# Layer 0 of a sparse graph stack: another order for the sign check, the ranges, the turned weights and the reciprocal

## The chip, the core and the metric

The kernel runs on one NeuronCore of a Trainium2 chip. A core has four engines that compute, each with its own instruction stream: TensorE (PE, matrix products and transposes through the array; its weight loads are shown as PEld), VectorE (DVE), ScalarE (ACT) and GpSimd (POOL). SyncE (SP) issues most of the transfers between the chip's memory (HBM) and the on-chip memory (SBUF); GpSimd issues the gathers. TensorE writes into PSUM, from where ScalarE and VectorE read. The engines meet at semaphores only; each works through its own instructions in the order in which the program lists them.

The metric is the device time of one execution in microseconds (us), the median of several runs; less is better.

## The reference

Four graph layers follow one another, each with a residual and a layer norm over rows of 512 numbers. The graph has 2708 nodes, and `adj` is a 2708 x 2708 matrix with about four entries per row besides its diagonal, all positive. Cut to what matters, with `ln` for the layer norm:

```python
# layer 0
e2 = (adj @ x) * (diag + 1)
x = ln(x + (x - e2) @ w0 + b0)
# layer 1: attention from two score columns and gates from the neighbour sums
h = x @ W_sa;  s = h @ a_left, h @ a_right
e = where(adj != 0, exp(-leaky_relu(s_i + s_j)), 0)
x = ln(x + sigmoid(gate_a * (e @ h) / (sum(e) + 1e-5) + gate_b * (adj @ (x @ W_gc) + b)))
# layer 2
inc = adj + (adj > 0) / sqrt(count of the row)
x = ln(x + (inc @ x) / sum(inc))
# layer 3: adj scaled by the degrees on both sides
x = ln(x + tanh(D A D x @ W.T + b))
```

## The kernel before

The kernel does not multiply by the dense matrix. It finds the entries of each block of columns of the transposed matrix, makes lists of them, gathers the rows of x that they name, and adds them with small matrix products. Where a list could not hold what was found, or a value was negative, a dense program would run instead; with this input it doesn't. All that the change touches is the phase for layer 0 inside `sparse_stack`, written as an order by hand (`manual_schedule`): each engine works through the instructions in exactly the order of the Python calls.

Two tilings run through this phase. The search and the sums work on *blocks*: NB = 24 blocks of R = 113 nodes. The projections and norms work on *windows*: KB = 22 windows of 128 rows. Blocks are smaller than windows, so in some steps no new window is complete. `window_at` maps a step to its window: steps 1 to 7 have windows 0 to 6, step 8 has none, 9 to 16 have 7 to 14, 17 has none, then 18 on.

The calls, with the line of the instruction in the profile:

- `find(i, parts)` (VectorE): each block has four segments (parts); MAX8 (L858) takes the eight largest values of each row, MATCH_VALUE_LOAD and FIND_INDEX8 (L860) their places. Segments 0 and 1 have 678 columns, 2 and 3 have 565. `search(n)` does the next n parts of a running list that starts at block 3; at a block's last part it also does `count` and issues the load of the block three further on.
- `negatives(i)` (ScalarE, L845): the sign check, one pass over the block's 2486 columns whose result (`negs`) is read only at the end of the phase. It must be listed before the load that overwrites the block.
- `count(i)` (VectorE, L872 to L882): the totals of each row. `starts(i)`: TensorE adds the totals of the rows ahead (L889), then ScalarE makes `ahead` (L892), `middle` (L894) and `q` (L896). `ranges(i)` (VectorE, L901) and `mark(i)` (VectorE, L908) make the selection matrix, `fetch(i)` (TensorE, L913, eight products) applies it, `pick(i)` (VectorE, L922 to L953) reads the edges from it, and its four gathers (GpSimd, L600) follow, with `nvalue` (ScalarE, L956).
- `values0(i)` (ScalarE, L966 and L967, eight activations) spreads the edges' values, `sums0(i)` (TensorE, L613, `l0a`) adds the gathered rows, `inputs0(i)` (VectorE, L979 to L984) and `turn_u(i)` (TensorE L1064, ScalarE L1073) prepare the block for the projection.
- For a window: `project0` (TensorE, L584, `o_l`), `bias0` (VectorE, L990), `residual0` (VectorE L1000, ScalarE L1005 to L1009: mean, squares, root), `norm0` (VectorE's reciprocal L1017, then ScalarE L1018 and L1019). One step later, for layer 1: `turn_x` (TensorE L575, ScalarE L577), `next0` (TensorE L584, `h`, ScalarE L1034 to L1039, then copies of rows by SP), `rest0` (TensorE L584, `hb`) and `store0` (ScalarE L1052, then SP).
- Once in the phase, the score columns that `next0` needs beside W_sa: `gate_columns` (L805 to L811), `turn_w(k)` (TensorE L819, ScalarE L821, four of them), `times_a(k)` (TensorE, L827), `score_rows` (ScalarE, L835), `score_columns` (TensorE L841, ScalarE L842).
- `keep_busy(n)` (TensorE, L797, `unread`): products that nobody reads, two passes of 512 columns each.

The phase begins with blocks 0 to 2 by hand, and then a loop runs over steps k = 0 to 25. Step k lists, in this order: `turn_x`; `ranges`, `mark` and `fetch` of block m = k + 2; `project0` of the step's window; one part of the search; `pick(m)`; one part; `residual0` and `norm0`; `next0`; `values0(m)`; the rest of the search; `sums0(k+1)` and `inputs0(k+1)`; `rest0` with `starts(m+1)` in its middle; `turn_u(k+1)`. A step has four parts of the search; three steps ahead of each step without a window have five, the step without a window ("bare") two and the one after it three. At the end of a plain step k the search stands at block k + 3 complete, and after the three longer steps it is up to three parts further.

Transfers on SP are issued in program order. TensorE's and ScalarE's buffers for transposes (`ps_tr`) are two, those for products (`ps_o`) three.

Of the kernel before, what the change touches and what calls it, by code (L numbers as in the profile page):

```python
# [19 lines left out]
EC = 4  # L20
# [427 lines left out]
def sparse_stack(  # L448
# [29 lines left out]
    nc = tc.nc  # L478
    N, D = x.shape
# [3 lines left out]
    NB = (N + R - 1) // R  # L483
# [3 lines left out]
    WG = 2 * D + 8  # L487
# [160 lines left out]
    with ExitStack() as phase:  # L648
# [144 lines left out]
        def keep_busy(n):  # L793

            o = ps_o.tile([P, D], FP, tag="o", name="unread")
            for _ in range(n):
                nc.tensor.matmul(o, lhsT=ident, rhs=iota_t, start=True, stop=True)  # L797
# [46 lines left out]
        def negatives(i):  # L844
            nc.scalar.activation(  # L845
                nojunk, abuf[i % NA].rearrange("p b i -> p (b i)"), AF.Relu, scale=-1.0,
                accum_out=negs[:, i : i + 1],
            )
# [143 lines left out]
        def project0(w):  # L992
            o0[w] = project(window_uT.pop(w), wrows(w), w0_sb, f"l0_{w}")
# [145 lines left out]
            )  # L1139
        w_gc_sb = load_w(w_gc, "w_gc_sb", first)  # L1140
        spread_rows()
        keep_busy(3)
        clear_diagonal(2)
        pick(0)
        values0(0)
        find(1, (1,), values=False)
        find(1, (2, 3))
        count(1)
        starts(1)
        keep_busy(2)  # L1150
        find(2, (0,), places=False)
        ranges(1)
        mark(1)
        fetch(1)
        negatives(2)
        nc.scalar.memzero(gflat[1])
        nc.scalar.memzero(gflat[2][:, KB * R + 3 * D :])
        find(2, (0,), values=False)
        find(2, (1,), places=False)
# [6 lines left out]
        find(2, (2, 3))  # L1166
        load_adj(5)
        count(2)
        values0(1)
        sums0(0)  # L1170
        starts(2)
        keep_busy(2)
        inputs0(0)
        turn_u(0)
        load_diagonal(4, NB - 1 - 4, R)
        load_diagonal(NB - 1, 1, rows(NB - 1))
        ba_bc = load_row(ba, "ba_bc", n=1)
# [9 lines left out]
        def search(n):  # L1187

            for _ in range(min(n, len(to_find))):
                b, g = to_find.pop(0)  # L1190
                if g == 0:
                    negatives(b)
                find(b, (g,))
                if g == 1 and b + 1 < NB:
                    clear_diagonal(b + 1)
                if g == NG - 1:
                    count(b)
                    if b + NA < NB:
                        load_adj(b + NA)
# [6 lines left out]
        for k in range(NB + 2):  # L1206
            m = k + 2
            w, wx, rest = window_at.get(k), window_at.get(k - 1), window_at.get(k - 1)
            bare = 2 < k < NB and w is None
            after = 2 < k < NB and wx is None  # L1210
            parts = 4
            if any(t not in window_at for t in (k + 1, k + 2, k + 3)) and 2 < k < NB - 4:
                parts = 5
            if bare:
                parts, rest = 2, None
            if after:
                parts, rest = 3, window_at[k - 2]
            if wx is not None and k <= NB:
                turn_x(wx)
            if m < NB:  # L1220
                ranges(m)
                mark(m)
                fetch(m)
            if w is not None:
                project0(w)
            if unstored:
                store0(unstored.pop())
            if k == 0:
                gate_columns()
                turn_w(0)  # L1230
                turn_w(1)
            search(1)
            if m < NB:
                pick(m)
                own[m] = load_own(m)
            if w is not None:
                bias0(w)
            search(1)
            if w is not None:
                residual0(w)  # L1240
            if k + 1 in window_at:
                load_window(window_at[k + 1])
            if w is not None:
                norm0(w)
            if k == 2:
                score_columns()
            if wx is not None and not bare:
                next0(wx)
            if m < NB:
                values0(m)  # L1250
            search(parts - 2)
            if k + 1 < NB:
                sums0(k + 1)
                inputs0(k + 1)
            if k + 2 == NB:
                worst = check_lists()
                for i in range(4):
                    load_own1(i)
            if k == 0:
                times_a(0)  # L1260
                turn_w(2)
                times_a(1)
            if k == 1:
                turn_w(3)
                times_a(2)
                times_a(3)
                score_rows()
            if bare:
                next0(wx)
            if rest is not None:  # L1270
                rest0(rest, lambda: turn_x(w) if k == NB else starts(m + 1) if m + 1 < NB else None)
                unstored.append(rest)
            elif m + 1 < NB:
                starts(m + 1)
            if k + 1 < NB:
                turn_u(k + 1)
            if k == NB:
                tell(worst)
                for i in range(4, NO):
                    load_own1(i)  # L1280
# [562 lines left out]
```

## Time and profile before

| | us |
|---|---|
| median of three runs | 1010.21 (1008.12 to 1011.41) |
| profiled execution, its own time | 992.9 |
| its span, first to last instruction | 991.2 |
| layer 0's phase within it | about 0 to 427 |
| mean granted TensorE clock | 0.968 |
| one plain step of layer 0, fetch to fetch | 15.74 |
| steps 5, 6, 7, 8, 9 | 16.30, 16.79, 16.95, 11.21, 14.50 |
| steps 14, 15, 16, 17, 18 | 16.31, 16.80, 16.95, 11.20, 13.66 |

A step's length is taken from the start of its first `fetched` product (L913) to that of the next step; the fetch of step k is that of block k + 2. Steps 0 to 3 begin at 40.17, 51.31, 69.97 and 89.95 us.

In the lines of the profile, L860 is line 860 of the kernel; `out<-in` names the tiles; xN is the number of instructions. In a timeline the first two numbers are the start and the length in us, and the brackets at the end say how long the engine had been idle before the instruction and whose end released it. A chain of waits is followed back from the last instruction to what each step had waited for.

### The profile page before, as it was taken

The page shows a single profiled execution, that of the slowest core. Times are in us where ns is not written, and L with a number is a line of the kernel's source. Part 1 is how long each engine was busy: PE and PEld are TensorE (multiplying, and loading weights), DVE is VectorE, ACT ScalarE, POOL GpSimd, SP SyncE. Part 2 cuts the span into 40 slices and gives each one's busy share as a digit, 9 for nine tenths or more (in the row PEclk, how much of TensorE's full clock was granted, in tenths as well). Part 3 has the DMA queues.
Part 4 walks back from the last instruction along what each step waited for, and adds up shares of the span by engine and source line. Part 5 has one row for each costly group of instructions (what it writes and reads, how often), then busy time and mean ns, then how long its engine had stood idle before and what let it go on. Part 6 is the DMA issues. An engine that isn't in the chain of part 4 may idle for free.

```text
span 991.2 us, 11201 instructions
## 1 busy us (share of the span) xinstructions
PE 899.3 (91%) x2973; PEld 494.5 (50%) x2973; DVE 686.4 (69%) x1803; ACT 530.0 (53%) x1219; POOL 473.0 (48%) x538
## 2 busy tenths in 40 slices
PE   7879999899998999999888888889888889999994
PEld 3335555555555555557666667633333334444441
DVE  7876888788887872138878878858787625655543
ACT  5765767667767664346776777415545412222222
POOL 3313131331313321046666767467777468776640
PEclk8979999999999999989999999989999999999998
DMA  9986877878778544378999998357777556555531
GB/s 237 302 210 173 210 216 195 236 220 223 213 214 219 163 131 123 118 231 294 299 317 283 323 299 279 93 158 211 221 219 211 159 151 181 169 169 163 168 109 32
DMA packets 133516, 201.70 MB, mean 203 GB/s; under 512 B 82456, under 2 KB 82502, under 8 KB 133445
## 3 DMA queue, kind: packets, MB, share of 16 engines
q0 software_dynamic: 36864, 111.73, 38.2%
q1 hardware_dynamic: 96581, 89.18, 31.8%
q8 instruction: 26, 0.43, 0.2%
q14 instruction: 45, 0.37, 0.1%
HBM read 181.83 MB, written 27.80 MB: 211 GB/s over the span
## 4 chain that ended last, share of the span: by engine, by line
PE 50%; DMA 16%; DVE 13%; ACT 10%; issue 6%; POOL 5%; SPq 0%; POOLq 0%; DVEq 0%; ACTq 0%
DMA gath<-table,source 15%; PE o_l L584 13%; PE l3a L613 8%; PE hb L584 5%; PE h L584 5%; PE l0a L613 4%; POOL gath L600 4%; PE l2a L613 4%; ACT s L967 2%; PE unread L1527 2%; DVE where_all L860 2%; ACT nojunk L845 2%; PE l1s L1404 2%; DVE rec_all L858 2%; PE fetched L913 1%
## 5 line engine op out<-in xcount | busy, mean ns | idle before, releaser
L600 POOL DMA_INDIRECT gath<-table,source x288 | 315.9, 1097 | 154.6 <-issue 64.0
L600 POOL DMA_INDIRECT gath<-in_x_dram,source x96 | 97.3, 1014 | 242.4 <-issue 204.5
L1404 PE MATMUL l1s<-gath,s 128*113 128x256 f32 (+3 forms) x384 | 96.6, 407 | 22.6 <-DVE l1b L1434 22.3
L613 PE MATMUL l2a<-gath,s_left 128*113 128x512 f32 (+1 forms) x192 | 95.7, 617 | 16.7 <-DMA gath<-table,source 14.5
L1404 PEld LDWEIGHTS l1s<-gath,s 128*113 128x113 f32 (+1 forms) x384 | 70.9, 189 | 48.4 <-DVE l1b L1434 29.7
L613 PE MATMUL l3a<-gath,s 128*113 128x512 f32 (+1 forms) x192 | 88.4, 602 | 3.6 <-DMA gath<-table,source 3.6
L584 PE MATMUL o_l<-shared,uT_l 128*113 128x512 f32 (+1 forms) x192 | 86.5, 593 | 0.7 <-ACT uT_l L577 0.7
L1414 PE MATMUL l1e<-gath,e 128*113 128x257 f32 (+3 forms) x384 | 87.0, 379 | 0.0
L613 PE MATMUL l0a<-gath,s 128*113 128x512 f32 (+1 forms) x192 | 86.3, 592 | 0.0
L584 PE MATMUL hb<-w_gc_sb,uT_x 128*128 128x512 f32 (+1 forms) x176 | 83.3, 601 | 0.0
L584 PE MATMUL o_l<-w_sb,uw 128*128 128x512 f32 (+1 forms) x176 | 82.4, 612 | 0.2
L584 PE MATMUL h<-w_sa_sb,uT_x 128*128 128x259 f32 (+1 forms) x352 | 81.0, 382 | 1.3 <-ACT w_sa_sb L842 1.3
L584 PEld LDWEIGHTS h<-w_sa_sb,uT_x 128*128 128x128 f32 (+1 forms) x352 | 64.8, 185 | 22.0 <-issue 8.0
L1414 PEld LDWEIGHTS l1e<-gath,e 128*113 128x113 f32 (+1 forms) x384 | 68.1, 177 | 15.2
L1762 ACT ACTIVATE y<-l3v,mv_l 113x512 f32<-113x512 f32 (+1 forms) x24 | 19.5, 813 | 87.3 <-DVE mv_l L1758 87.3
L613 PEld LDWEIGHTS l2a<-gath,s_left 128*113 128x113 f32 (+1 forms) x192 | 30.2, 179 | 71.7 <-DMA gath<-table,source 45.3
L584 PEld LDWEIGHTS o_l<-shared,uT_l 128*113 128x113 f32 (+1 forms) x192 | 33.9, 177 | 48.9 <-issue 47.1
L613 PEld LDWEIGHTS l3a<-gath,s 128*113 128x113 f32 (+1 forms) x192 | 32.6, 180 | 42.2 <-issue 39.3
L613 PEld LDWEIGHTS l0a<-gath,s 128*113 128x113 f32 (+1 forms) x192 | 33.8, 177 | 38.9 <-issue 37.7
L1291 DVE TENSOR_SCALAR s<-niota_r,nrow,edges 128x113 f32<-128x113 f32 x192 | 51.8, 349 | 0.0
L860 DVE FIND_INDEX8 where_all<-rec_all,shared 128x8 uint32<-128x678 f32 (+1 forms) x64 | 51.2, 800 | 0.0
L858 DVE MAX8 rec_all<-shared 128x8 f32<-128x678 f32 (+1 forms) x64 | 50.8, 795 | 0.0
(239 smaller groups left out, 1556.4 us busy)
## 6 DMA issues: line engine op xcount, KB each, us to landing
shared<-in_adj_dram SPq DMA_DIRECT2D x14, 1186.5 KB
table<-st SPq DMA_DIRECT2D x21, 514.5 KB
gath<-in_adj_dram SPq DMA_DIRECT2D x7, 1186.5 KB
shared<-table SPq DMA_DIRECT2D x16, 448.0 KB
gath<-in_x_dram SPq DMA_DIRECT2D x21, 256.0 KB
xi<-in_x_dram SPq DMA_DIRECT2D x23, 224.0 KB
table<-xr SPq DMA_DIRECT2D x23, 224.0 KB
table<-y SPq DMA_DIRECT2D x23, 224.0 KB
```

Of the source, the lines that this page charges most:

```text
L584: nc.tensor.matmul(o, lhsT=uT[:, f, :r], rhs=w[:, f, :], start=(f == 0), stop=(f == DB - 1))
L600: nc.gpsimd.indirect_dma_start(out=g[:, c, :n], out_offset=None, in_=src[:, :], in_offset=bass.IndirectOffsetOnAxis(ap=source[:, i, c : c ...
L613: nc.tensor.matmul(agg[:r, :], lhsT=s[:, c, :r], rhs=g[:, c, off : off + D], start=(c == 0), stop=(c == EC - 1),)
L845: nc.scalar.activation(nojunk, abuf[i % NA].rearrange("p b i -> p (b i)"), AF.Relu, scale=-1.0, accum_out=negs[:, i : i + 1],)
L858: nc.vector.max(out=top, in_=seg)
L860: nc.vector.max_index(out=where_all[:, i, g * 8 : (g + 1) * 8], in_max=top, in_values=seg)
L967: nc.scalar.activation(spread0[i][:, c, :], t, AF.Relu, bias=edges[:, i, c, 1:2], scale=nvalue[:, i, c : c + 1],)
L1291: nc.vector.tensor_scalar(s[:, c, :], niota_r, nrow[:, i, c : c + 1], edges[:, i, c, 1:2], op0=ALU.is_equal, op1=ALU.mult,)
L1404: nc.tensor.matmul(sum_s[i][:r, k, : at.stop - at.start], lhsT=s[:, c, :r], rhs=g[:, c, at], start=(c == 0), stop=(c == EC - 1),)
L1414: nc.tensor.matmul(sum_e[i][:r, k, k : k + at.stop - at.start], lhsT=e[:, c, :r], rhs=g[:, c, at], start=(c == 0), stop=(c == EC - 1),)
L1527: nc.tensor.matmul(o[:, :cols], lhsT=ident, rhs=bg_bc[:, :cols], start=True, stop=True)
L1762: nc.scalar.activation(y[:r, :], v[:r, :], AF.Identity, bias=mv[:r, 3:4], scale=mv[:r, 2:3])
```

## The change

No computation changes; instructions are listed elsewhere, and some are left out.

- Of the filler products, `keep_busy(3)` ahead of block 2's diagonal and the second `keep_busy(2)` are left out.
- `values0(0)` moves from ahead of block 1's last parts to after `starts(1)`; `values0(1)` from ahead of `sums0(0)` to after `turn_u(0)`.
- The zeroing of the second gather buffer leaves out the stretch that holds the windows.
- `gate_columns`, `turn_w(0)` and `turn_w(1)` move from step 0 to before `inputs0(0)`; `times_a(0)` and `turn_w(2)` go to the first part of step 0, `times_a(1)` and `turn_w(3)` to its end; `times_a(2)` and `times_a(3)` to before `project0` of step 1, `score_rows` after its `store0`, and `score_columns` from step 2 to the end of step 1.
- `negatives` no longer goes with a block's first part in `search`; each step k lists `negatives(k + 3)` after its `store0`.
- One part of the search moves ahead of `norm0` in steps with more than two parts.
- In a bare step `starts(m + 1)` is listed before `next0`.

```diff
         spread_rows()
-        keep_busy(3)
         clear_diagonal(2)
         pick(0)
-        values0(0)
         find(1, (1,), values=False)
         find(1, (2, 3))
         count(1)
         starts(1)
+        values0(0)
         keep_busy(2)
...
         negatives(2)
-        nc.scalar.memzero(gflat[1])
+        for a, b in ((0, EC * D), (EC * D + 4 * D + 12, EC * WG)):
+            nc.scalar.memzero(gflat[1][:, a:b])
...
         count(2)
-        values0(1)
         sums0(0)
         starts(2)
-        keep_busy(2)
+        gate_columns()
+        turn_w(0)
+        turn_w(1)
         inputs0(0)
         turn_u(0)
+        values0(1)
...
                 b, g = to_find.pop(0)
-                if g == 0:
-                    negatives(b)
                 find(b, (g,))
...
+            if k == 1:
+                times_a(2)
+                times_a(3)
             if w is not None:
                 project0(w)
+            if k == 0:
+                times_a(0)
+                turn_w(2)
             if unstored:
                 store0(unstored.pop())
-            if k == 0:
-                gate_columns()
-                turn_w(0)
-                turn_w(1)
+            if k + 3 < NB:
+                negatives(k + 3)
+            if k == 1:
+                score_rows()
             search(1)
...
+            if parts > 2:
+                search(1)
             if w is not None:
                 norm0(w)
-            if k == 2:
-                score_columns()
             if wx is not None and not bare:
                 next0(wx)
             if m < NB:
                 values0(m)
-            search(parts - 2)
+            search(parts - 3)
             if k + 1 < NB:
                 sums0(k + 1)
                 inputs0(k + 1)
+            if k == 1:
+                score_columns()
...
             if k == 0:
-                times_a(0)
-                turn_w(2)
                 times_a(1)
-            if k == 1:
                 turn_w(3)
-                times_a(2)
-                times_a(3)
-                score_rows()
             if bare:
+                starts(m + 1)
                 next0(wx)
-            if rest is not None:
+            elif rest is not None:
```

## The prediction

> **What bounds the kernel now.** I read the page, then a table of windows, the chain of waits in order of time, and the timeline of the steps that the chain named. The page's first part: TensorE is busy 91% of the span.
>
> ```profile
> PE 899.3 (91%) x2973; PEld 494.5 (50%) x2973; DVE 686.4 (69%) x1803; ACT 530.0 (53%) x1219; POOL 473.0 (48%) x538
> ```
>
> Layer 0 ends near 427 us. The windows say where TensorE is not full in it (busy us of PE, PEld, DVE, ACT, POOL, then granted clock, DMA share, GB/s):
>
> ```profile
> 20.00:40.00 20.00, 16.73 (x39) 7.05 (x38) 14.59 (x43) 14.80 (x29) 7.14 (x9) 0.76 1.04 333
> 60.00:80.00 20.00, 13.66 (x42) 7.38 (x40) 14.21 (x38) 12.88 (x30) 5.38 (x7) 0.74 0.66 174
> 100.00:120.00 20.00, 20.00 (x71) 11.41 (x70) 16.26 (x44) 14.46 (x38) 4.29 (x5) 1.00 0.75 195
> 160.00:200.00 40.00, 36.26 (x131) 20.85 (x130) 30.93 (x82) 28.28 (x69) 11.77 (x13) 0.96 0.80 224
> ```
>
> A plain step (100 to 120) is TensorE end to end; work taken off other engines there gains nothing. Two places have slack: the first 80 us, at three quarters of the clock, and the stretch around each step without a window (k=8, 17). The chain of waits (start, length) names ScalarE's sign check in the stretch:
>
> ```profile
> 65.90 1.87 PE w_a L827 x2
> ...
> 133.96 2.26 ACT nojunk L845 x2
> 150.55 2.26 ACT nojunk L845 x2
> 167.69 2.26 ACT nojunk L845 x2
> 174.95 2.35 ACT nojunk L845 x2
> 182.69 1.48 PE fetched L913 x8
> ```
>
> It returns at 272.79, 289.39, 306.54 and 313.79. The timeline of the start, with the idle time before each instruction and who ended it:
>
> ```profile
> 26.88 0.19 DVE L901 SCALAR_TENSOR_TENSOR rec_all<-ahead,far 128x32 f32<-128x32 f32 x1 [4.29 <-ACT ahead L892]
> ...
> 36.29 3.52 PE L797 MATMUL unread<-gath,ident 128*128 128x512 f32 x4
> ...
> 65.90 1.87 PE L827 MATMUL w_a<-w_saT,a_cols 128*2 128x512 f32 x2 [5.18 <-ACT w_saT L821]
> ...
> 80.19 2.02 PE L584 MATMUL h<-w_sa_sb,uT_x 128*128 128x259 f32 x8 [1.34 <-ACT w_sa_sb L842]
> ```
>
> VectorE stands 4.3 us for ranges(1), TensorE 5.2 us for the turned weight, 1.3 us for the score columns. And step 8's end, where the list of block 11 is late:
>
> ```profile
> 179.39 0.28 PE L889 MATMUL fetched<-totals,under 128*128 128x1 f32 x2
> ...
> 181.02 0.29 ACT L892 ACTIVATE ahead<-fetched,totals 128x1 f32<-128x1 f32 x1
> ...
> 182.69 1.48 PE L913 MATMUL fetched<-rec_all,q 128*128 128x96 f32 x8 [2.57 <-DVE q L908]
> ```
>
> **What the Trainium skill says.** "TensorE: Matmul & The Clock Gate", Part 1: an idle window of about 3.4 us halves the clock, a busy one restores it. The trace agrees: 512-column passes start 0.43 us apart, but 0.85 at 17 to 26, 37 to 40 and 68 to 74 us. The same page, architectural detail: ScalarE and VectorE are strict FIFO, matmuls keep their order; so each wait below stops all behind it, as the 4.29 us did. "ScalarE: Activation LUTs", What ACT_TABLE_LOAD costs: 0.833 ns per element; the zeroing of 4128 took 3.63 us, so 2048 is an estimated 1.9. "DMA: Bandwidth & Descriptors", Issuing engines are not separate DMA queues: both queues share 16 engines; their share is 1.04 at 20 to 40 us.
>
> **The start, part by part.** keep_busy(3) held TensorE from 20.94 to 26.4 while block 1's totals lay ready at 21.58; starts(1) waited, then ranges(1). It goes, and values0(0) (8 activations, 3.4 us) steps behind starts(1). For block 0 totals to ranges took 0.93 us (11.55 to 12.48), so ranges(1) comes at 22.6, after the find in between. But keep_busy(2), which stays, now runs at half clock, 4 x 0.85 from 22.3 to 25.7, ahead of fetch(1). So pick(1), 29.69 before, comes about 26.9. The smaller zeroing frees ScalarE 1.7 us earlier.
>
> From pick(1) VectorE is nearly full: its 6.5 us to count(2) and 2.2 us of inputs0(0) end at 35.6 instead of 38.38. The second keep_busy(2) (3.52 us) goes; gate_columns and two turn_w (9 small transposes, 1.3 us) take its place, hidden in TensorE's wait for inputs0(0). They need w_rows and w_sa, issued at 25.5 to 29.4; no row shows a landing; the DMA rate dips only near 37, so they land between 29.4 and 37. I take 34: first in their queue. TensorE now stands at gate_columns until then, with turn_u(0) and fetch(2) queued behind; at 37 turn_u(0) would be 1.2 us later. fetch(2): 36.6 instead of 40.17, at half clock (2.02 us as at 69.97), so pick(2) 38.8 instead of 41.25.
>
> Now ScalarE is full: from 34.8, two gate copies 0.35, three weight turns 1.7, turn_u 0.55, values0(1) 3.4 (moved here, past starts(2), so sums0(1) begins near 40.4 instead of 42.24), negatives(3) 2.3, nvalue 0.2, values0(2) 3.4, the fourth turn 0.6, starts(3) 1.2: 48.5, with 0.5 of mark, fetch(3) at 49.3 instead of 51.31. Two times_a (4 passes, 2.0) now precede project0(0), which so ends at 55.8, as before (55.9): here the move costs its full price. ScalarE's score_rows waits for them until 52.4; behind it stand nvalue(3) and residual0's statistics, needed at 56.8, so nothing is lost. But bias0(0) no longer waits for its window, since SP's loads begin 2.5 us sooner (load_adj(4) follows pick(1)'s gathers on POOL), so residual0(0) is at 56.0 instead of 57.46. The reciprocal, 3.4 us later as now (a 1.28 us table load in it), is at 59.4; one find (1.55) lies inside this wait. Behind it norm0 and values0(3) end at 64.1, the score copy 64.3, starts(4), mark(4) at 65.5 instead of 69.43: the 5.2 us stall is gone, since the turned weights were done 15 us before. turn_u, turn_x, fetch(4) at 66.2 instead of 69.97; clock still half as now; project0(1) ends at 72.9 if the clock returns at 70.7, 75.1 if at 74.1; next0(0) follows unbroken, 3.5: 76.4 or 78.6, before 82.21. Gain 3.6 to 5.8; a clock lost once more near 50 costs 1.4. Bounds 2 to 5.8; I take 5.0.
>
> **Plain steps.** The third part before the reciprocal: find 1.55 in a wait of 1.44, so 0.1 later. In step 3 (fetch 89.95) ScalarE waits 0.76 before ahead, and mark ends 0.85 before fetch: 1.6 us cover. Cost 0; without cover 0.1 a step. The sign check of a plain step stays where it was, after store0; no transfer moves.
>
> **The two stretches.** Steps 5, 6, 7 take 16.30, 16.79, 16.95 by their first fetch, against 15.74. Causes: the second sign check, 2.45 us, between values0 and ahead; and VectorE, 15.1 us of work plus 1.44 of waiting in step 6. After: the check sits behind store0, where ScalarE waits up to 4 us for residual0 anyway; VectorE's wait is filled. In steps 6 and 15 the third part ends a block (count 0.93), so the reciprocal is 1.05 late, within the 1.6; there the block load (2.9 us of SP's issue) also goes ahead of next0's row copies, which layer 1 alone reads. So 15.74, 15.82, 15.82: 0.56+0.97+1.13 = 2.66.
>
> Step 8, 11.21: values0(10) can begin at 174.95 instead of 177.21; starts(11) comes before next0, straight after sums0(9) (176.0), so ahead waits only for values0, 178.3, q 179.5, mark 180.0; TensorE's own row is fetch 1.13, sums 3.43, starts 0.15, h 3.5, turn_u 0.58 = 8.8. I take 9.0: 2.2. next0's h lies 0.15 later, copies then after ahead; their readers come in step 9.
>
> Step 9: three parts only, and the third ends block 12, so the reciprocal is at 8.8 after fetch (find 1.75, pick 1.85, bias 0.65, find 1.5, residual 0.7, find and count 2.4) instead of 8.46; nothing covers: 14.75 against 14.50, −0.25. Step 18: 8.65 against 7.62, −1.05.
>
> Stretch one 2.66+2.2−0.25 = 4.6; two, with 16.31, 16.80, 16.95, 11.20 and 13.66: 2.68+2.2−1.05 = 3.8.
>
> **Sum.** 5.0+4.6+3.8 = 13.4 us. All of it lies before layer 0's last rows, which layer 1 gathers, so it passes on. Span 991.2 to 977.8; the profiled execution 992.9 to 979.5; the three runs' median 1010.21, 17.3 above it, to 996.8. I say 997.
>
> **Rivals.** *Clock lost* (chance 0.15): with ten filler passes gone, TensorE stays at half clock through 40 to 54 us; sums0(1) takes 3.6 more, four times_a passes 1.8: 5.4, the start gains nothing. 8.4 left: 1002. For it: PEclk 0.76 despite filler. Against: the sums themselves make busy windows.
>
> *The start falls together* (0.08): every gap and half-clock loss after 36 us goes (2.1+5.2+1.3 idle, 3.4 of filler, 6 of clock: 18); with a third kept back 12, plus 8.4: 990. Against: between 40 and 80 us VectorE is busy 77%, ScalarE 66%, and each waits for the other.
>
> *Reciprocal* (slower, 0.05): the reciprocal queues behind a find and sometimes a count; if it came 2.3 us later in each of 18 steps, 0.75 over the 1.6 cover would eat 13.5 us and it begins to lose; at 2.6, 1014. Against: I count 0.1 and 1.05.
>
> *Swallowed* (0.06): layer 1's chain is 15% gathers; if these, not the rows, set its start, nothing changes: 1010. Against: the last rows' copies run up to 427, then layer 1 starts at once.
>
> **Numbers.** Forecast 0.66 (992 to 1001); faster 0.66+0.15+0.08 = 0.89, within 0.3% (3 us, about what this measurement can tell) 0.06, slower 0.05. The range 991 to 1003.5 takes in the forecast, the lost clock and half of the falling-together case; 0.15 is left out.
>
> **What shows it.** Right: nojunk gone from the chain; steps 5 to 7 at 15.8, 8 and 17 near 9; no 5.2 us wait at w_a; step 3's fetch near 85. Wrong: PEclk under 0.7 at 20 to 60, TensorE waiting at w_rows_t, plain steps over 15.9, or steps 9 and 18 over 16.

## The result and the profile after

| | before | after |
|---|---|---|
| median, us | 1011.41 (1007.05 to 1012.6, 7 runs) | 1001.58 (996.88 to 1003.22, 7 runs) |
| ratio, with 95% interval | | 0.991 (0.9885 to 0.9935) |
| profiled execution, its own time | 992.9 | 1001.58 |
| its span | 991.2 | 999.7 |

The change gains 9.8 us (6.6 to 11.6 by the interval) where 13.4 were forecast. The two profiled executions stand the other way round: that of before is quicker than all its timed runs. So the two spans can't be compared. Layer 0 can: its last `hb` product ends at 427.19 us before and at 419.34 after, 7.85 us earlier. Layers 2 and 3, which the change doesn't touch, take 128.5 and 191.5 us in the profile of before, 136.5 and 199.4 in that of after. Those 16 us get a paragraph of their own below.

The first part of the page, after: the engines' busy time, share of the span and instructions.

```profile
PE 898.5 (90%) x2963; PEld 498.5 (50%) x2963; DVE 685.7 (69%) x1803; ACT 527.9 (53%) x1220; POOL 472.4 (47%) x538
```

The table of windows, after (busy us of PE, PEld, DVE, ACT and POOL, then granted clock, DMA share, GB/s):

```profile
20.00:40.00 20.00, 15.81 (x49) 8.97 (x47) 16.41 (x46) 13.96 (x33) 7.42 (x9) 0.67 1.09 342
60.00:80.00 20.00, 16.00 (x57) 10.29 (x56) 15.23 (x43) 15.03 (x38) 4.42 (x5) 0.83 0.69 188
100.00:120.00 20.00, 20.00 (x81) 12.21 (x80) 16.72 (x47) 14.95 (x35) 4.31 (x5) 1.00 0.90 245
160.00:200.00 40.00, 36.31 (x138) 21.17 (x137) 31.30 (x89) 28.38 (x71) 13.23 (x14) 1.00 0.74 214
300.00:340.00 40.00, 36.28 (x116) 19.96 (x115) 28.64 (x81) 26.57 (x66) 13.53 (x15) 0.91 0.61 177
```

The start is better filled at 60 to 80 (16.00 of 20, 13.66 before). The stretch is not: TensorE is as idle at 160 to 200 as it was (36.31 of 40, 36.26 before). The idle time has moved, and the chain of waits of after (start, length, what) says where to:

```profile
164.90 2.26 ACT nojunk L845 x2
...
167.64 2.45 SPq L677
...
170.84 6.72 DMA gath<-in_x_dram
177.59 0.69 DVE gath L990
...
182.57 0.17 DVE st_l L1017
...
187.31 0.73 ACT q L896
188.61 1.13 PE fetched L913 x8
```

Of the four sign checks of the first stretch, three are gone from the chain. One stays, at 164.90, and something new hangs on it: SP's block load (L677; its first part, L673, stands just ahead), behind that the load of the window (6.72 us from issue to landing), and on the window `bias0` (L990), the reciprocal (L1017), `q` and step 9's end. The timeline of before, for the check that this block load waits for, the step's first fetch, the two loads and the same `bias0`:

```profile
167.60 2.26 ACT L845 ACTIVATE nojunk<-shared 128x2486 uint8<-128x2486 f32 x1
...
171.48 1.13 PE L913 MATMUL fetched<-rec_all,q 128*128 128x96 f32 x8 [0.58 <-DVE q L908]
...
173.00 0.40 SPq L673 DMA_DIRECT2D shared<-in_adj_dram  x1
...
177.67 0.35 SPq L569 DMA_DIRECT2D gath<-in_x_dram  x1
...
186.07 0.69 DVE L990 TENSOR_TENSOR gath<-gath,gath 128x512 f32<-128x512 f32 x1
```

and of after, with the idle time in brackets:

```profile
163.62 1.03 PE L913 MATMUL fetched<-rec_all,q 128*128 128x96 f32 x8
...
164.78 2.29 ACT L845 ACTIVATE nojunk<-shared 128x2486 uint8<-128x2486 f32 x1
...
167.18 0.40 SPq L673 DMA_DIRECT2D shared<-in_adj_dram  x1
...
170.84 0.35 SPq L569 DMA_DIRECT2D gath<-in_x_dram  x1
...
177.59 0.69 DVE L990 TENSOR_TENSOR gath<-gath,gath 128x512 f32<-128x512 f32 x1 [2.17 <-DMA gath<-in_x_dram]
```

Before, 8.4 us lay between the window load's issue and its use, and nobody waited. After, `bias0` wants the window 4.6 us after the issue (177.59 less the wait of 2.17, less 170.84). Two things shortened the time: step 8 is 2.8 us shorter, and against its step's fetch the block load comes 2.0 us later (3.56 instead of 1.52) and the window load behind it 1.0 later, because the block load waits for the sign check of the block that it overwrites. Before, that check ran at 167.60, ahead of the step's fetch at 171.48; now it runs at 164.78, behind the fetch at 163.62.

Step lengths of all profiles, from fetch to fetch, in us ("5-7" is three steps together; the start is the fetch of step 3; layer 0's end is that of its last `hb`):

| kernel | start | 5-7 | 8 | 9 | 10 | 14-16 | 17 | 18 | 19 | layer 0's end |
|---|---|---|---|---|---|---|---|---|---|---|
| before | 89.95 | 50.04 | 11.21 | 14.50 | 15.84 | 50.06 | 11.20 | 13.66 | 15.84 | 427.19 |
| before, again | 88.83 | 50.05 | 11.20 | 14.50 | 15.84 | 50.05 | 11.20 | 14.51 | 15.84 | 426.88 |
| after | 84.91 | 47.23 | 8.42 | 16.56 | 15.84 | 47.23 | 8.42 | 17.11 | 18.74 | 419.34 |
| after, again | 85.92 | 47.23 | 8.42 | 16.45 | 15.84 | 47.23 | 8.42 | 16.68 | 17.41 | 418.48 |
| window first | 85.14 | 47.23 | 8.42 | 14.31 | 17.53 | 47.22 | 8.42 | 14.31 | 15.84 | 413.31 |
| check a step earlier | 85.64 | 48.54 | 9.00 | 14.39 | 15.84 | 48.54 | 9.00 | 14.39 | 17.51 | 417.73 |
| reciprocal old | 87.44 | 48.57 | 8.55 | 16.22 | 15.84 | 48.59 | 8.54 | 16.76 | 16.13 | 421.51 |
| starts old | 86.91 | 47.23 | 10.05 | 14.88 | 15.84 | 47.23 | 10.07 | 15.25 | 15.84 | 418.17 |
| check old | 84.33 | 50.43 | 10.53 | 14.51 | 17.54 | 50.44 | 10.52 | 14.40 | 17.54 | 425.12 |
| start old | 90.00 | 47.23 | 8.42 | 17.00 | 17.54 | 47.23 | 8.42 | 17.16 | 17.45 | 425.33 |
| window first, values early | 84.77 | 47.23 | 8.42 | 12.26 | 15.74 | 47.23 | 8.42 | 12.26 | 15.74 | 406.96 |
| the same, diagonal later | 86.10 | 47.23 | 8.42 | 12.26 | 15.74 | 47.23 | 8.42 | 12.26 | 15.74 | 408.29 |

The expected times below start from the first table's medians. The experiments came in three groups, each on one chip, with runs of the kernel before on that chip: median 1012.15 us (12 runs) for the first four, 992.81 (9) for the next four, 1007.66 (25) for the last two. So times are compared within a group, by their ratio to the kernel before, and layer 0 by the table.

### The profile page after: what moved, and what is told of

The parts are those of the page before. It is cut to its first block, busy times and chain, and to the rows that moved or that the text cites. A ratio compares the mean times of both kernels' runs of the same rounds, so it can differ in the third digit from the quotient of the medians.

```text
span 999.7 us, 11191 instructions
## 1 busy us (share of the span) xinstructions
PE 898.5 (90%) x2963; PEld 498.5 (50%) x2963; DVE 685.7 (69%) x1803; ACT 527.9 (53%) x1220; POOL 472.4 (47%) x538
## 4 chain that ended last, share of the span: by engine, by line
PE 66%; DVE 11%; DMA 9%; issue 4%; ACT 3%; POOL 3%; another core or an unknown queue 2%; SPq 1%; POOLq 0%; DVEq 0%; ACTq 0%
PE o_l L584 15%; PE l3a L613 9%; PE l2a L613 8%; PE hb L584 7%; PE h L584 7%; DMA gath<-table,source 7%; PE l0a L613 6%; PE unread L1530 3%; PE l1s L1407 3%; POOL gath L600 2%; PE fetched L913 2%; PE l1e L1417 2%; DVE where_all L860 2%; DMA gath<-in_x_dram 1%
## 5 line engine op out<-in xcount | busy, mean ns | idle before, releaser
L1407 PE MATMUL l1s<-gath,s 128*113 128x256 f32 (+3 forms) x384 | 93.6, 398 | 23.9 <-DVE l1b L1437 23.4
L613 PE MATMUL l2a<-gath,s_left 128*113 128x512 f32 (+1 forms) x192 | 93.5, 629 | 3.5 <-DVE s_left L1570 2.0
L613 PE MATMUL l3a<-gath,s 128*113 128x512 f32 (+1 forms) x192 | 90.4, 614 | 3.6 <-DMA gath<-table,source 3.6
L1407 PEld LDWEIGHTS l1s<-gath,s 128*113 128x113 f32 (+1 forms) x384 | 68.7, 184 | 49.5 <-DVE l1b L1437 32.2
L613 PE MATMUL l0a<-gath,s 128*113 128x512 f32 (+1 forms) x192 | 86.9, 593 | 0.2 <-DMA gath<-in_x_dram,source 0.2
L1530 PE MATMUL unread<-bg_bc,ident 128*128 128x512 f32 x88 | 47.1, 655 | 21.9 <-remote 17.2
L613 PEld LDWEIGHTS l2a<-gath,s_left 128*113 128x113 f32 (+1 forms) x192 | 34.4, 191 | 53.3 <-issue 44.5
L1739 DVE SCALAR_TENSOR_TENSOR l3v<-o_l,d_inv,b_bc 113x512 f32<-113x512 f32 (+1 forms) x25 | 18.1, 729 | 58.5 <-PE o_l L584 55.1
## 6 DMA issues: line engine op xcount, KB each, us to landing
shared<-in_adj_dram SPq DMA_DIRECT2D x14, 1186.5 KB
gath<-in_adj_dram SPq DMA_DIRECT2D x7, 1186.5 KB
```

What stands on the lines that cost most here:

```text
L613: nc.tensor.matmul(agg[:r, :], lhsT=s[:, c, :r], rhs=g[:, c, off : off + D], start=(c == 0), stop=(c == EC - 1),)
L1407: nc.tensor.matmul(sum_s[i][:r, k, : at.stop - at.start], lhsT=s[:, c, :r], rhs=g[:, c, at], start=(c == 0), stop=(c == EC - 1),)
L1530: nc.tensor.matmul(o[:, :cols], lhsT=ident, rhs=bg_bc[:, :cols], start=True, stop=True)
L1739: nc.vector.scalar_tensor_tensor(v[:r, at], o[:r, at], d_inv[:r, i : i + 1], b3_bc[:r, at], op0=ALU.mult, op1=ALU.add,)
```

## The experiments

The expectations call it the *SP theory* that the window load is late because it stands on SP behind a block load that waits for the moved sign check. Where they say that a run undoes a part, the rest is the changed kernel.

### Window first

In the bare step the window load goes to the head of the step, ahead of the block load.

```diff
+            if bare and k + 1 in window_at:
+                load_window(window_at[k + 1])
             if wx is not None and k <= NB:
                 turn_x(wx)
...
-            if k + 1 in window_at:
+            if k + 1 in window_at and not bare:
                 load_window(window_at[k + 1])
```

> The changed kernel, with the load of the next window listed at the head of a step without a window (8 and 17), ahead of the block load on SP. In the changed kernel VectorE's bias0 stands 2.17 us in step 9 and 2.72 us in step 18 for that load. Theory SP (the window's load comes late because it stands on SP behind the block load, which waits for the moved sign check): no such wait, steps 9 and 18 fall from 16.56 and 17.11 to 14.7, step 19 from 18.74 to 15.8 because the clock no longer drops; layer 0's last product from 419.3 to about 412.2; time 994.5. Theory reciprocal (these steps are long because the reciprocal stands behind a find and a count): they stay over 16, time 1001. Theory DMA (the load is slow because of the gathers, wherever it is listed): the wait stays at 1 to 2 us.

Measured: 997.52 us (993.86 to 1004.44, 5 runs), ratio 0.9842 (0.9805 to 0.9879). Its timeline:

```profile
160.99 0.47 SPq L569 DMA_DIRECT2D gath<-in_x_dram  x1
...
175.58 0.68 DVE L990 TENSOR_TENSOR gath<-gath,gath 128x512 f32<-128x512 f32 x1
...
180.56 0.16 DVE L1017 RECIPROCAL st_l<-st_l 128x1 f32<-128x1 f32 x1
...
186.59 1.45 PE L913 MATMUL fetched<-rec_all,q 128*128 128x96 f32 x8 [1.89 <-DVE q L908]
```

With the load issued at 160.99 `bias0` no longer waits; steps 9 and 18 take 14.31, 2.3 and 2.8 us less than in the changed kernel. Layer 0 ends 6.0 us earlier. That is the SP theory's result, within half a microsecond a step; the time is 3 us above the 994.5 expected, and the other two theories, by which the steps or the wait would have stayed, fall. With 14.6 us from issue to use the run would hide a slow load too: how long the load takes behind a block load is read from the traces, not from this run. What is left of step 9 is 1.89 us in which TensorE waits for `q`; the clock halved after it (187.2 to 190.7) and step 10 paid 1.7 us. After the same pause in step 18 it did not. The expectation had step 19 lose no clock, which holds, and did not foresee step 10.

### The check a step earlier

The sign check of the block that a bare step would check is listed one step sooner, at the end of ScalarE's `values0`.

```diff
-            if k + 3 < NB:
+            if k + 3 < NB and not bare:
                 negatives(k + 3)
...
+            if 2 < k < NB - 4 and k + 1 not in window_at:
+                negatives(k + 4)
             search(parts - 3)
```

> The changed kernel, with the sign check of blocks 11 and 20 listed in steps 7 and 16 behind values0, instead of in steps 8 and 17. Theory SP: the block load in step 8 is issued about 2.1 us earlier, so the window's too, and bias0 in step 9 waits under 0.3 us: step 9 14.7, step 18 near 15; steps 7 and 16 become 0 to 1 us longer; layer 0's last product 413 to 415, time 995 to 997. Theory reciprocal: steps 9 and 18 unchanged. Theory short step (step 8 has become too short for the load, wherever the check is): the wait falls by less than 1 us.

Measured: 1003.21 us (996.82 to 1007.57, 9 runs), ratio 0.9911 (0.988 to 0.9941): the same as the changed kernel. Steps 9 and 18 came down to 14.39, as the theory has it, without a wait at `bias0`. Layer 0 ends at 417.73, not at the 413 to 415 expected. The expectation forgot what the check does in its new place. Timeline of step 7's end:

```profile
161.79 2.26 ACT L845 ACTIVATE nojunk<-shared 128x2486 uint8<-128x2486 f32 x1
...
164.05 0.24 ACT L892 ACTIVATE ahead<-fetched,totals 128x1 f32<-128x1 f32 x1
...
165.66 1.13 PE L913 MATMUL fetched<-rec_all,q 128*128 128x96 f32 x8 [1.15 <-DVE q L908]
```

The check stands ahead of `ahead`, as the second check did in the kernel before; step 7 takes 17.06 instead of 15.74, step 8 0.58 more. Most of what the window gives back, `q` takes: of the 2.2 us in step 9 and the 2.7 in step 18, 1.9 each time go to the two steps before. Neither this place nor the changed kernel's is free for a pass of 2.3 us.

### The reciprocal in its old place

```diff
-            if parts > 2:
-                search(1)
             if w is not None:
                 norm0(w)
...
-            search(parts - 3)
+            search(parts - 2)
```

> The changed kernel, with the third part of the search back behind norm0 in all steps. Theory SP: steps 9 and 18 lose only the reciprocal's lateness, 1.0 us each: 15.5 and 16.1; steps 5 to 7 and 14 to 16 rise from 15.74 towards 16.5, since VectorE's 15.1 us of work get their 1.44 us of waiting back; time 1001 to 1003. Theory reciprocal: steps 9 and 18 return to 14.5 and 13.7, time 997. My prediction's claim that plain steps don't move: 15.74.

Measured: 1002.48 us (1001.07 to 1002.85, 4 runs), ratio 0.991 (0.9875 to 0.9944), not told apart from the changed kernel by its time. The table tells more. Steps 9 and 18 keep their wait for the window (16.22, 16.76; 2.35 us at `bias0` in step 9): the reciprocal's place is not the cause. Steps 5 to 7 lose 1.34 of the 2.81 us. And the start is 2.5 us later in this one profile; the eight profiles with the changed start and the third part lie between 84.33 and 86.91, by their clock. In the two that are compared here the clock was half for the same 3.4 us near 50. TensorE's totals product (L889) in step 1, first of this kernel, then of the changed one:

```profile
65.39 0.59 PE L889 MATMUL fetched<-totals,under 128*128 128x1 f32 x2 [4.22 <-DVE totals L877]
```

```profile
63.38 0.38 PE L889 MATMUL fetched<-totals,under 128*128 128x1 f32 x2 [1.94 <-DVE totals L877]
```

VectorE stood 2.72 us for the root in this kernel and then had two parts and a count still before it; in the changed one a part lies inside that wait (1.21 left) and this product comes 2.0 us sooner.

### The kernel before, again

> The kernel before, unchanged, to see how much of a profile repeats. The first profile of it had a span of 991.2 us, below all of its timed runs. Layer 0's steps should repeat within 0.1 us (steps 5 to 9 16.30, 16.79, 16.95, 11.21, 14.50; last product at 427.2). If the 17 us between span and timed runs arise in layers 2 and 3, these are longer here than 128.5 us (first to last product of layer 2) and 191.5 us (layer 3).

Measured: 1013.04 us (one run), span 1011.3. Layer 0 repeats to 0.3 us at its end; layer 2 takes 137.6 us and layer 3 200.8, as long as after the change. The table of windows for a stretch inside layer 2, the first profile of before, this one, and the changed kernel's:

```profile
655.00:785.00 130.00, 113.82 (x261) 41.87 (x259) 98.93 (x272) 62.03 (x114) 99.66 (x95) 0.99 0.73 211
```

```profile
655.00:785.00 130.00, 108.82 (x249) 43.38 (x247) 91.09 (x249) 55.31 (x104) 93.66 (x91) 0.91 0.69 196
```

```profile
655.00:785.00 130.00, 109.65 (x248) 43.91 (x247) 91.24 (x254) 59.73 (x112) 92.89 (x90) 0.92 0.68 200
```

The same kernel on the same input gets 0.99 of the clock in one and 0.91 in the other. One step of layer 0 does not repeat: step 18 takes 14.51 here and 13.66 in the first profile, because the clock was half from 322.0 to 325.4 us here and full there. The 16 us between the first two profiles are not the change's.

### Window first, values early

Window first, and in the step after a bare one the eight activations of `values0` listed ahead of the residual's statistics.

```diff
+            if after:
+                values0(m)
             search(1)
             if w is not None:
                 residual0(w)
...
-            if m < NB:
+            if m < NB and not after:
                 values0(m)
```

> The window load at the head of the bare step, as in the run with that edit alone, and in the step after a bare one the eight activations that spread the edges' values are listed before the statistics of the residual. In that step ScalarE stood idle 2.96 us before the statistics, and the values, which need only the picked edges, came after the norm and put `ahead` at 184.97, so that TensorE stood 1.9 us before the fetch. Theory (with the window there in time, what is left of steps 9 and 18 is ScalarE's order behind the late reciprocal, the term that the prediction priced at 0.25 and 1.05 us): steps 9 and 18 take about 12.4 instead of 14.31, the pause is too short to cost the clock, layer 0 ends near 408 instead of 413.3, and the whole comes to about 993.5. Rival (the steps are now held by the list's way over VectorE, not by ScalarE): steps 9 and 18 stay at 14.0 to 14.3, and the whole near 997.5.

Measured: 971.09 us (969.48 to 973.15, 5 runs), ratio 0.9787 (0.9769 to 0.9805): faster than the kernel before, and by a ratio clear of the changed kernel's 0.991. Steps 9 and 18 take 12.26; layer 0 ends at 406.96, 12.4 us before the changed kernel and 20.2 before the kernel before, which is the gain in time (21.7) to 1.5 us. The 971 itself belongs to this chip; on 0.9787 of the first table's 1011.41 it would be an estimated 990. ScalarE in step 9 of the window-first kernel, the statistics and then, behind the norm and the values, `ahead`:

```profile
178.40 0.20 ACT L1005 ACTIVATE st_l<-st_l 128x1 f32<-128x1 f32 x1 [2.96 <-DVE l0v L1000]
...
184.97 0.24 ACT L892 ACTIVATE ahead<-fetched,totals 128x1 f32<-128x1 f32 x1
```

With the values in that idle time, `ahead` comes at 181.72. The windows of its two stretches:

```profile
160.00:200.00 40.00, 40.00 (x157) 23.74 (x155) 34.79 (x96) 31.39 (x79) 13.20 (x14) 1.00 0.83 234
300.00:340.00 40.00, 40.00 (x152) 24.22 (x151) 35.29 (x95) 30.15 (x77) 16.30 (x17) 1.00 0.67 199
```

TensorE is busy 40.00 of 40.00 us in both, at full clock. The rest of steps 9 and 18 was ScalarE's order: the values stood behind a norm that stood behind a late reciprocal.

### `starts` in its old place

```diff
             if bare:
-                starts(m + 1)
                 next0(wx)
-            elif rest is not None:
+            if rest is not None:
```

> The changed kernel with one part undone: in the bare step `starts` of the next block is listed after `next0` again. SP theory (steps 8 and 9 together end at a time that the window load sets, so what step 8 gains by the early `starts`, step 9 waits for): step 8 goes from 8.42 to about 10.3, step 9 falls by the same, and steps 8 and 9 together stay within 0.5 us of 24.98; layer 0 ends within 1 us of 419.3 and the time is within 1.5 us of the changed kernel's 1001.6. Rival (the early `starts` is worth its 2.2 us, and the wait for the window is another matter): 8 and 9 together come to 26.5 to 27, layer 0 ends near 423, and the time is about 1005.

Measured: 985.29 us (983.81 to 987.2, 4 runs), ratio 0.9927 (0.9906 to 0.9949). Step 8 is 10.05 and step 9 14.88, together 24.93 against 24.98; 17 and 18 are 25.32 against 25.53. The wait at `bias0` in step 9 has shrunk from 2.17 to 0.39:

```profile
179.52 0.69 DVE L990 TENSOR_TENSOR gath<-gath,gath 128x512 f32<-128x512 f32 x1 [0.39 <-DMA gath<-in_x_dram]
```

So in the changed kernel the early `starts` is worth nothing by itself: the window's landing sets the end of the pair, and what step 8 gains, step 9 waits. The two ratios, 0.9927 here and 0.991, lie within each other's intervals; layer 0 even ends 1.2 us earlier, since no clock is lost in step 19 (15.84), which more than makes up for a later start. With the window first, step 8 keeps its 8.42 and step 9 doesn't grow; a kernel with the window first and `starts` in its old place was not run, so what the early `starts` is worth there is not measured.

### The start in its old order

The part before the loop and the score columns' work as before; sign check, third part and bare step as changed.

```diff
+        keep_busy(3)
         clear_diagonal(2)
         pick(0)
+        values0(0)
...
-        gate_columns()
-        turn_w(0)
-        turn_w(1)
+        keep_busy(2)
...
-            if k == 1:
-                times_a(2)
-                times_a(3)
             if w is not None:
                 project0(w)
...
```

> The changed kernel with the old order in everything before the loop and the old places of the score columns' work; the sign check, the third part and the bare step as changed. If the prediction's working of the start is right (early ranges, early turned weights, fewer filler passes), its 5.0 us are lost: step 3's fetch near 89.9 and the time near 1006.6. Rival (half of it is the third part of the search ahead of the reciprocal, which in step 1 fills the wait for the table load; undoing that part alone moved step 3's fetch by 2.5 us): step 3's fetch near 87.4, layer 0's end near 421.9, and the time near 1004.

Measured: 987.47 us (985.16 to 989.34, 4 runs), ratio 0.9939 (0.9915 to 0.9963). Step 3's fetch is at 90.00: the whole gain of the start is gone, and the rival (87.4) falls. Undoing the third part ahead of the reciprocal took half of the start's gain (reciprocal old), but without the early ranges and weights it gives nothing: the two don't add. Why stays open, and so does how the gain divides among the start's other edits, which were undone together only. Layer 0 ends 6.0 us later than in the changed kernel. The times tell less: the two ratios differ by 0.0029, some 3 us, and their intervals overlap.

### The sign check in its old place

```diff
                 b, g = to_find.pop(0)
+                if g == 0:
+                    negatives(b)
                 find(b, (g,))
...
-            if k + 3 < NB:
-                negatives(k + 3)
```

> The changed kernel with the sign check back beside a block's first search part. SP theory (the moved check holds the block load, and with it the window load behind it on the same queue): steps 9 and 18 have no wait for the window and take 14.3 to 14.8; steps 5 to 7 lose the half of their gain that undoing the third part alone left, so 16.1 to 16.3 each, step 8 goes to about 10.3; steps 5 to 9 together come to about 73.5 against 72.2, layer 0 ends near 421, and the time is near 1003.5. Rival (the check's move does the harm and nothing else): steps 5 to 9 together 70 or less, and a time near 997.

Measured: 988.37 us (987.35 to 988.58, 4 runs), ratio 0.9952 (0.9934 to 0.997). Its timeline, the second check of step 8 and `bias0` of step 9:

```profile
169.71 2.26 ACT L845 ACTIVATE nojunk<-gath 128x2486 uint8<-128x2486 f32 x1
...
180.15 0.68 DVE L990 TENSOR_TENSOR gath<-gath,gath 128x512 f32<-128x512 f32 x1
```

Nothing waits for the window, and step 9 is 14.51, as the theory has it. But steps 5 to 9 come to 75.47, not 73.5; before they were 75.75. Without the moved check the third part ahead of the reciprocal gains nothing in steps 5 to 7 (50.43, before 50.04). So the check's move is worth 3.3 us in the first stretch and 2.6 in the second (steps 14 to 18 take 75.36 here, 72.76 in the changed kernel) even with the wait that it brings; the rival, that it does only harm, falls. Steps 10 and 19 take 17.54 here: pauses of 2.00 and 1.89 us before their first fetch cost the clock.

### The changed kernel again, and the diagonal later

> The changed kernel, nothing altered, with a profile of its own. If what was read in layer 0 belongs to the order of the work: steps 3 to 7 at 15.74, 8 and 17 at 8.42, 9 and 18 between 16.5 and 17.2 with a wait of about 2 us for the window at bias0, step 3's fetch at 84.5 to 86, and a ratio to the kernel before of 0.990 to 0.993. If the chip makes the 16 us by which layers 2 and 3 differed between the first two profiles, both are as long here as in the kernel before on the same chip, and the gain is what layer 0 gives: 8 to 10 us. Rival (the change lengthens layers 2 and 3): they are 6 us or more longer than in the kernel before of this chip.

Measured: 1001.9 us (999.01 to 1007.33, 18 runs), ratio 0.9939 (0.9917 to 0.9962): 5.8 us on this chip, less than expected. The steps repeat; 9 and 18 again wait 2.04 and 2.29 us for the window. Layers 1 to 3 take 579.7 us (998.14 less 418.48). No profile of the kernel before was taken on this chip; its median less the 1.7 us that lie around a span, less 426.9 for layer 0, gives an estimated 579.1 for the same layers. This profile is a quick one, though; the changed kernel's median, taken the same way, gives an estimated 581.6. By the interval of the ratio the gain is 3.8 to 8.4 us, of which layer 0 alone would give 8.4. So a lengthening by 6 us or more is not seen; one of a few microseconds is not ruled out here.

The last run is the fastest kernel with two diagonal loads and two bias rows moved on SP behind step 0's window load.

```diff
-        load_diagonal(4, NB - 1 - 4, R)
-        load_diagonal(NB - 1, 1, rows(NB - 1))
-        ba_bc = load_row(ba, "ba_bc", n=1)
-        bb_bc = load_row(bb, "bb_bc", n=1)
...
             if k + 1 in window_at and not bare:
                 load_window(window_at[k + 1])
+            if k == 0:
+                load_diagonal(4, NB - 1 - 4, R)
+                load_diagonal(NB - 1, 1, rows(NB - 1))
+                ba_bc = load_row(ba, "ba_bc", n=1)
+                bb_bc = load_row(bb, "bb_bc", n=1)
```

> The two edits of the fastest run so far, and the last two loads of the diagonal and the two bias rows moved on SP's queue from before step 0 to behind step 0's window load; no computation is touched. In the changed kernel these four issues held SP from 44.32 to 49.68 and bias0(0) then waited 1.86 us for its window. Theory (that wait is on the start's path): bias0(0) starts at 52.9, residual0(0) 0.5 to 1.9 us earlier, since TensorE's product for it ends at 57.67, and step 3's fetch comes at 83.5 to 84.3; the time falls by 0.5 to 1.5 us. Rival (the product o_l, not the window, ends last, so the wait cost nothing beyond 0.04 us): bias0(0) is earlier, residual0(0) stays at 57.7, step 3's fetch stays at 84.8 to 85.1, and the time is that of the run without this edit, 0.979 of the kernel before.

Measured: 984.76 us (983.14 to 985.88, 6 runs), ratio 0.9761 (0.972 to 0.9802), the same as without the edit within the intervals. `bias0(0)` no longer waits (53.53), but `residual0(0)` then waits 2.91 us for TensorE's product and starts at 58.87, not 57.7; step 3's fetch is at 86.10. The clock was half from 48.3 to 55.1 in this profile, until that product began (55.13); in the changed kernel from 50.5 to 53.9. The wait at `bias0(0)` was not on the path; the product was, and the clock's phase moves it by more than this edit could.

## Why the prediction was right, and where it was not

The time fell inside the range and on the forecast's side; it is 4.6 us above the 997.0. That it lies inside is in part luck: layer 0 gave 7.84 of the 13.4 us, the upper part of the range was there for a clock lost in the start, and on another chip the same change gained 5.8. By the terms of its sum, from the two first profiles:

| term | forecast | measured |
|---|---|---|
| start | 5.0 | 5.04 |
| steps 5 to 7, 14 to 16 | 2.66, 2.68 | 2.81, 2.83 |
| steps 8, 17 | 2.2, 2.2 | 2.79, 2.78 |
| step 9 | -0.25 | -2.06 |
| step 18 | -1.05 | -3.45 |
| step 19 | 0 | -2.90 |
| sum, layer 0 | 13.4 | 7.84 |

- **Start: right, by a path that was partly wrong.** Ranges(1) came at 22.92 (forecast 22.6), fetch(1) at 26.00 (25.7), fetch(2) 37.25 (36.6), fetch(3) 49.41 (49.3). Then "bias0(0) no longer waits for its window" failed, and TensorE's product was late too. It ended at 57.67, not at 55.8: the clock was half from 50.5 to 53.9, under the two `times_a`, which took 3.57 us and not 2.0. The prediction had named this loss as possible ("a clock lost once more near 50"). In the second profile of the changed kernel `bias0(0)` does not wait. The lines of the first:

```profile
54.73 0.69 DVE L990 TENSOR_TENSOR gath<-gath,gath 128x512 f32<-128x512 f32 x1 [1.86 <-DMA gath<-in_x_dram]
...
57.71 0.69 DVE L1000 SCALAR_TENSOR_TENSOR l0v<-o_l,gath 128x512 f32<-128x512 f32 x1 [0.54 <-PE o_l L584]
...
73.49 3.66 PE L584 MATMUL h<-w_sa_sb,uT_x 128*128 128x259 f32 x16
```

  `residual0(0)` is 1.7 us later than worked out (56.0), fetch(4) 1.2 (67.45 for 66.2). `next0`'s products end at 77.15, still within the 76.4 to 78.6 worked out: the clock came back at 71.0, the early one of the two times that the prediction left open. The 5.2 us stall at `w_a` is gone. From profile to profile the new start moves between 84.3 and 86.9 and the old one between 88.8 and 90.0, so the 5.04 is good to a microsecond or two, and that it meets 5.0 so closely is chance.
- **Plain steps: right.** 15.74 throughout; the later reciprocal cost nothing there.
- **Steps 5 to 7: right**, and for the two causes named. The runs add how they depend on each other: the check's move alone gives 1.47 of the 2.81 us (undoing the third part loses 1.34), while the third part gives nothing without the check's move (undoing that loses all).
- **Steps 8 and 17: right mechanism, undersized.** 9.0 was taken though TensorE's own row came to 8.8; it is 8.42, TensorE end to end.
- **Steps 9 and 18: this step failed.** The prediction priced them by the reciprocal behind a find and a count alone. That term was fair: with the window in time both are 14.31, where 14.75 and 14.7 were forecast. Its two sizes, 0.25 and 1.05, differ by an accident: step 18 of the profile read was 13.66 because the clock stayed full there, and in the second profile of before it is 14.51, so that the loss in step 18 is 2.60 against that one. What it left out is the window. It wrote that "the sign check of a plain step stays where it was" and "no transfer moves", and did not follow the check in the bare step, where it went from ahead of the fetch to behind it. SP runs its queue in order, so the window load stood behind a block load that stood behind the check, while the step that had hidden it grew 2.8 us shorter. Its own sign for being wrong, "steps 9 and 18 over 16", came true. Measured, the mechanism is shown by the window-first run; the share of each of its two causes (1.0 us of later issue, 2.8 of earlier need) is read from two traces.
- **Step 19: not in the sum.** The fetch that ends step 18 waited 2.69 us, and the clock halved during that wait:

```profile
324.44 2.02 PE L913 MATMUL fetched<-rec_all,q 128*128 128x96 f32 x8 [2.69 <-DVE q L908]
```

  It stayed so from 323.6 to 330.4 and cost 2.9 us (1.6 in the second profile). The rival *clock lost* put the loss into the start, where the gain stood; its 1002 was close for another reason.
- **The median's place.** The forecast took what it read in one profile, of 992.9 us, off a median 17 us higher. Layer 0 allows that: it ends at 427.19 and 426.88 us in the two profiles of before. The other layers of the first profile were quicker than in the timed runs; its time and its clock are like those of the kernel before in the second group of runs (992.81), but on which chip it was taken is not known.

## What to carry over

When an instruction is moved on one engine, list what its end releases, and then what stands behind that on the queue of transfers: here a 2.3 us check that nobody needs until the end held a load, and a second load behind it. When a step gets shorter, every transfer that was hidden in it has that much less time, so check the distance from issue to use (8.4 us before, 4.6 after, where the load took 6.7). And a part's worth depends on what else is in: the early `starts` was worth nothing while the window came late, and the third part of the search nothing without the check's move. With the window first, and the values moved into ScalarE's idle time, the stretch is TensorE from end to end and layer 0 gains 20 us, not 8.

## What the runs showed of the hardware

- **The same kernel differed by 2% from group to group.** The kernel before took 992.81, 1007.66 and 1012.15 us (medians) in the three groups, each on another chip. Between its two profiles layer 0's end differs by 0.3 us, layer 2 by 9.1 and layer 3 by 9.3, at a granted clock of 0.99 against 0.91 inside layer 2. Why some executions lose the clock there was not tried.
- **A pause of about 2 us can cost the clock, or not.** "TensorE: Matmul & The Clock Gate", Part 1 of the Trainium skill, says that the clock is set by windows of about 3.4 us that run free of the program. The runs agree: in the profile of after, every change of the clock in layer 0 (at 16.4, 26.6, 33.4, 40.2, 50.5, 53.9, 64.1, 71.0, 323.6 and 330.4 us) lies on one grid of 3.41 us, though the work between them follows no such grid. Where a pause falls on that grid may then decide, beside its length; no run moved a pause alone. The same pause of 1.89 us before a fetch halved the clock in step 9 of the window-first kernel (1.7 us lost in step 10) and not in step 18; 2.68 us didn't in step 9 of the changed kernel, and 2.69 did in step 18, for 6.8 us instead of 3.4; the 2.56 us at the end of step 17 of the kernel before did in one profile and not in the other. The page speaks of an idle window; here pauses shorter than a window were enough, and how little work in a window counts as idle no run shows.
- **A window's load behind a block load took 6.2 to 7.1 us.** SP issued the window's 256 KB behind the block's 1186.5 KB and 226 KB of the block's own rows. In the changed kernel it landed 6.72 us after its issue (6.65 in step 17), and in all ten cases in which `bias0` waited for it, five profiles with two each, `bias0` began 6.2 to 7.1 us after the issue. In the start of the changed kernel, with smaller loads right ahead of it, the first window's 256 KB took 3.3 us (issued at 51.40, `bias0` at 54.73). The Trainium skill, "DMA: Bandwidth & Descriptors", Two DMAs through the same engine are not ordered, says that within one queue of an engine descriptors start in order; the traces agree with that as far as they go, and no run shows the same load with nothing ahead of it.
